# A decay in two factors and a fixed issue order for the first units of a state-space mixer on one Trainium2 core

## Chip, core and metric

The kernel runs on one core of a Trainium2 chip. The metric is the device time in microseconds (us). The engines are TensorE (PE, with its weight loads shown as PEld), VectorE (DVE), ScalarE (ACT), GpSimd (POOL) and SyncE (SP), which here only issues transfers.

## What is computed

Two layers, each an attention-like part and a feed-forward part with residuals and layer norms, over 1024 tokens (4 sequences of 256) of 512 features. The change lies in the second layer's first part, a state-space mixer with 128 heads of 64, 8 groups of state size 128, and chunks of 128 tokens, so two chunks a sequence:

```python
proj = hidden_states @ in_proj_w.T            # gate, hBC (x, B, C), dt
hBC = silu(causal_conv4(hBC) + conv_b)        # depthwise, 4 taps
dt = softplus(dt + dt_bias); A = -exp(A_log)
A_cumsum = cumsum(A * dt)                     # inside each chunk
L = exp(segment_sum(A * dt))                  # decay inside a chunk
Y_diag = (C.B * L) @ (x * dt)                 # a chunk on itself
states = (B * exp(A_cumsum[last] - A_cumsum)).T @ (x * dt)
Y_off = (C @ states of the chunk before) * exp(A_cumsum)
y = Y_diag + Y_off + D * x
out = (y * rsqrt(mean(y*y) + eps) * norm_w * silu(gate)) @ out_proj_w.T
```

With two chunks, only chunk 1 gets anything from before, and that comes from chunk 0. The kernel computes it without states, as a third block of C.B with its own decay. For a token l of chunk 1 and a token s of chunk 0 that decay is exp(cs1[l]) times exp(rev[s]), where cs is the running sum of A dt inside its chunk and rev[s] is the sum of A dt over the tokens of chunk 0 after s.

## The kernel before

Everything is float32. The mixer works through 72 **units**: for each of 8 groups one unit of B and C (units 0, 9, 18, ...), then 8 **pairs** of heads. The main loop at the end of the mixer runs over n, and each turn n does parts of four units:

- `stage_a(n)` projects unit n: seven products (`product`, L503) of two 128x128 by 128x512 matmuls, each of which the trace counts as two instructions. They go into the tiles pd, pa and pb, of a PSUM pool of four buffers (tag "in"). It is Strassen-like: the weights come in two 256 KB loads (win, L558 and L559), GpSimd makes four sums of them (wsum, L489 to L492), ACT copies partial results out of PSUM (`keep`, L514), and DVE adds them to later products (L526, L530, L533). Then DVE makes the causal convolution (`conv_silu`: one instruction L542 and three L546) and ACT the silu (L554). A unit of B and C has two convolutions, a pair has one, and its gate goes through silu on ACT (L591, L592).
- `load_sums(n)` loads the pair's running sums: cst, two rows of cs_d spread over all partitions, two buffers.
- `stage_t(n-1)`: for a unit of B and C, the products C.B of the group (ps_g and p1, L617 and L624), masked into gt by DVE (L634, L640) and ACT (L646). For a pair, transposes of x (ps_xt, L652), x dt (xdt, L655), and the decays in cst: L667 on DVE makes four blocks a head for chunk 0 on chunk 1 out of cst and rev, L671 on ACT eight blocks a head inside the chunks, then one exp over all of it (L675) and two products with gt on DVE (L677).
- `stage_c(n-2)`: ps_y, 16 matmuls a head pair of the blocks inside chunks (L692) and 8 from chunk 0 on chunk 1 (L700), both with xdt as weights; then D, the norm's weight and the gate on DVE (L708, L711), squares on ACT (L710) and their sum (L714).

The output projection (ps_p, L732) adds up to four pairs to two of eight token tiles in every turn, and DVE adds it to acc (L740, L742). The tiles ps_dt, ps_cs, ps_csT, ps_g, ps_xt and ps_y share one PSUM buffer (tag "mm2", one buffer); p1, ps_rev and ps_p share two ("mm1").

Ahead of the loop stands `time_steps`: the dt projection (L405), softplus as a series on DVE (L415 to L433, with a reciprocal, L425), and A dt (adt, L437). At the end of turn 1 `sums` makes the running sums (ps_cs, L445, copied to cs), rev (ps_rev, L454), the transposed sums (ps_csT, L464) and stores them to cs_d in DRAM (L467).

A scheduler orders the instructions of each engine at build time by their place in the program and by its own estimates; each engine then takes its queue in that order, and waits for data and for free buffers with semaphores. Nothing in the program fixes the order beyond the data's own dependencies.

Of the kernel before, what the change touches and what calls it, by code (L numbers as in the profile page):

```python
# [30 lines left out]
P = 128  # L31
# [20 lines left out]
def model_kernel(ctx: ExitStack, tc: tile.TileContext, a: dict, out: bass.AP):  # L52
# [299 lines left out]
    with ExitStack() as c1:  # L352
# [5 lines left out]
        class Psum:  # L358
            @staticmethod
            def tile(shape, dt, tag, name):  # L360
                return {"mm2": psum2, "mm1": psum1, "in": psumi}[tag].tile(shape, dt, tag=tag, name=name)

        wdt = cw.tile([P, KT, P], F32, tag="wdt", name="wdt")
        nc.sync.dma_start(out=wdt, in_=a["win"][T_DT])
# [18 lines left out]
        cs = cw.tile([P, NT, P], F32, tag="cs", name="cs")  # L383
        rev = cw.tile([P, NB, P], F32, tag="rev", name="rev")
        cs_d = dram.tile([P, NTOK], F32, tag="cs_d", name="cs_d")

# [8 lines left out]
        def time_steps():  # L395
# [7 lines left out]
            for t in range(NT):  # L403
                for k in range(KT):
                    nc.tensor.matmul(  # L405
                        flat(ps)[:, toks(t)],
                        lhsT=xnT[:, k, toks(t)],
                        rhs=wdt[:, k, :],
                        start=(k == 0),
                        stop=(k == KT - 1),  # L410
                    )
# [12 lines left out]
            nc.vector.tensor_scalar(r, u, 2.0, None, ALU.add)  # L424
            nc.vector.reciprocal(r, r)  # L425
            nc.vector.tensor_tensor(u, u, r, ALU.mult)
            nc.vector.tensor_tensor(s2, u, u, ALU.mult)
            nc.vector.tensor_scalar(r, s2, 1.0 / 15, None, ALU.mult)
            for n in (13, 11, 9, 7, 5, 3):
                nc.vector.scalar_tensor_tensor(r, r, 1.0 / n, s2, ALU.add, ALU.mult)  # L430
            nc.vector.scalar_tensor_tensor(r, r, 1.0, u, ALU.add, ALU.mult)
# [4 lines left out]
            nc.vector.tensor_scalar(na, na, -1.0, None, ALU.mult)  # L436
            nc.vector.tensor_tensor(adt, dt, bcast_mid(na, sh), ALU.mult)  # L437

            return adt

        def sums(adt):

            ps = Psum.tile([P, 2, 512], F32, "mm2", "ps_cs")
            for n in range(2):
                nc.tensor.matmul(  # L445
                    ps[:, n, :],
                    lhsT=tri_le,
                    rhs=adt[:, n * 4 : n * 4 + 4, :],
                    start=True,
                    stop=True,  # L450
                )
            nc.scalar.copy(cs, flat(ps).rearrange("p (t h) -> p t h", h=P))
            pr = Psum.tile([P, 512], F32, "mm1", "ps_rev")
            nc.tensor.matmul(  # L454
                pr,
                lhsT=tri_gt,
                rhs=adt.rearrange("p (b c) h -> p b c h", c=2)[:, :, 0, :],
                start=True,
                stop=True,
            )  # L460
            nc.scalar.copy(rev, pr.rearrange("p (b h) -> p b h", h=P))
            ps = Psum.tile([P, 2, 512], F32, "mm2", "ps_csT")
            for t in range(NT):
                nc.tensor.transpose(flat(ps)[:, toks(t)], cs[:, t, :], ident)  # L464
            csT = b2.tile([P, NTOK], F32, tag="xdt", name="csT")
            nc.scalar.copy(csT, flat(ps))
            nc.sync.dma_start(out=cs_d, in_=csT)  # L467

# [26 lines left out]
        def project(n, one, two):  # L495
# [4 lines left out]
            def product(ps, wt, tk, start=False):  # L500

                for k in range(2):
                    nc.tensor.matmul(  # L503
                        ps,
                        lhsT=wt[:, k, :],
                        rhs=tk[:, k, :],
                        start=start and k == 0,
                        stop=k == 1,
                        skip_group_check=not start,
                    )  # L510

# [17 lines left out]
            product(pd, v[:, 3], quarter(1, 1))  # L529
            nc.vector.tensor_tensor(one[:, 512:], pd, c2, ALU.add)  # L530
            yield
            product(pa, v[:, 2], tok[2])
            nc.vector.tensor_tensor(two[:, 512:], pa, c3, ALU.add)  # L533
            yield
# [34 lines left out]
        def prefetch(n):  # L569
            if n < len(units):  # L570
# [3 lines left out]
                weight_sums(n)  # L574

        def stage_a(n):
            kind, i = units[n]
# [3 lines left out]
            if kind == "bc":  # L581
                raw2 = xyp.tile([P, NTOK], F32, tag="xy", name=f"raw2_{n}")
                pa = yield from project(n, raw, raw2)
                nc.scalar.copy(raw2[:, :512], pa)
                conv_silu(raw, 64 + i, first)
                conv_silu(raw2, 72 + i, second)
                held[n] = [first, second]
            else:
                pa = yield from project(n, raw, second)
                conv_silu(raw, i, first)  # L590
                nc.scalar.activation(second[:, :512], pa, AF.Silu)  # L591
                nc.scalar.activation(second[:, 512:], second[:, 512:], AF.Silu)  # L592
                held[n] = {"xT": first, "sg": second}
# [3 lines left out]
        def load_sums(n):  # L597

            kind, j = units[n]
            if kind == "bc":  # L600
                return
            cst = b2.tile([P, 2, NT + NB, P], F32, tag="cst", name=f"cst{j}")
            nc.sync.dma_start(
                out=cst.rearrange("p h c l -> p h (c l)")[:, :, :NTOK],
                in_=cs_d[2 * j : 2 * j + 2, :].unsqueeze(0).to_broadcast([P, 2, NTOK]),
            )
            held[n].update(cst=cst)

        def stage_t(n):
            kind, i = units[n]  # L610
            if kind == "bc":
# [4 lines left out]
                for b in range(NB):  # L616
                    nc.tensor.matmul(  # L617
                        flat(ps)[:, b * SEQ : (b + 1) * SEQ],
# [4 lines left out]
                    )  # L623
                    nc.tensor.matmul(  # L624
                        p1[:, toks(b)],
# [25 lines left out]
            for t in range(NT):  # L651
                nc.tensor.transpose(flat(ps)[:, toks(t)], hd["xT"][:, toks(t)], ident)  # L652
            xdt = b2.tile([P, NT, P], F32, tag="xdt", name=f"xdt{j}")
# [5 lines left out]
                ALU.mult,  # L659
            )  # L660


            m = hd["cst"]
            for hh in range(2):
                h = 2 * j + hh
                for b in range(NB):
                    nc.vector.tensor_scalar(  # L667
                        m[:, hh, NT + b, :], m[:, hh, 2 * b + 1, :], rev[:, b, h : h + 1], -1.0, ALU.add, ALU.mult
                    )
                for c in range(NT):  # L670
                    nc.scalar.activation(  # L671
                        m[:, hh, c, :], m[:, hh, c, :], AF.Relu, bias=cs[:, c, h : h + 1], scale=-1.0
                    )
            mf = m.rearrange("p h c l -> p h (c l)")
            nc.scalar.activation(mf, mf, AF.Exp, scale=-1.0)  # L675
            for hh in range(2):
                nc.vector.tensor_tensor(mf[:, hh], mf[:, hh], gr.rearrange("p c l -> p (c l)"), ALU.mult)  # L677
            hd["xdt"] = xdt

        ys = []  # L680

        def stage_c(n):
            kind, j = units[n]
            if kind == "bc":
                return
            hd = held.pop(n)
            xdt, m = hd["xdt"], hd["cst"]
            py = Psum.tile([P, 2, 512], F32, "mm2", f"ps_y{j}")
            for c in range(NT):
                halves = [slice(hh * 64, (hh + 1) * 64) for hh in range(2)]  # L690
                for hh, e in enumerate(halves):
                    nc.tensor.matmul(  # L692
                        flat(py)[e, toks(c)],
# [5 lines left out]
                for hh, e in enumerate(halves if c % 2 else []):  # L699
                    nc.tensor.matmul(  # L700
                        flat(py)[e, toks(c)],
                        lhsT=xdt[:, c - 1, e],
                        rhs=m[:, hh, NT + c // 2, :],
                        start=False,
                        stop=True,
                    )
# [20 lines left out]
        def out_project(q, t, upto):  # L727
# [3 lines left out]
            for j in range(j0, upto):  # L731
                nc.tensor.matmul(  # L732
                    ps,
# [11 lines left out]
        prefetch(1)  # L745
        adt = time_steps()
        token_sums()
        for j in range(6):
            load_wout(j)
        added = 0  # L750
        for n in range(len(units) + 3):
            a_steps = stage_a(n) if n < len(units) else iter(())
            upto, q = len(ys), (len(ys) - 1) % PER_OUT
            fresh = upto > added
            next(a_steps, None)
            if fresh:
                out_project(q, 2 * q, upto)
            next(a_steps, None)
            if 0 <= n - 2 < len(units):
                stage_c(n - 2)  # L760
            next(a_steps, None)
            if fresh:
                out_project(q, 2 * q + 1, upto)
                behind[q] = added = upto
                load_wout(min(behind) + 5) if upto >= PER_OUT else None
            if 0 <= n - 1 < len(units):
                stage_t(n - 1)
            next(a_steps, None)
            if n == 1:
                sums(adt)  # L770
            if n < len(units):
                load_sums(n)
# [115 lines left out]
```

## Time and profile before

| what | value |
|---|---|
| three runs | 1883.59, 1884.53, 1885.9 us |
| median | 1884.53 us |
| profiled execution, its own time | 1885.57 us |
| span of its instructions | 1883.5 us |
| mean granted clock of TensorE | 0.988 |
| PE, DVE, ACT, POOL busy | 1840.0, 1396.1, 1068.8, 308.9 us |
| moved by DMA | 146.63 MB |
| cst, 64 loads of 1024 KB, median to landing | 4.7 us |

The profile is of one execution. A group of instructions has a line, an engine, an operation and its tiles; "idle before" is how long its engine stood still ahead of it and what ended that. A matmul of 128x512 is recorded with its pipeline's end, so four of them in a row last 1.88 us but start again every 1.715 us. The clock column gives the share of TensorE's full clock that was granted.

### The profile page before, as it was taken

How to read it: one execution, taken by the hardware profiler on the slowest of the kernel's cores; microseconds unless marked ns; L12 is line 12 of the kernel's file. 1: busy time of each engine (PE TensorE's matmuls, PEld its weight loads, DVE VectorE, ACT ScalarE, POOL GpSimd, SP SyncE). 2: the span in 40 equal slices, each digit the busy share in tenths (PEclk: the TensorE clock that was granted, in tenths of full speed). 3: DMA queues.
4: the chain of work that ended last, by engine and by line, in shares of the span. 5: the costliest groups of instructions: out<-in, count | busy, mean ns of one | idle time of the engine just before them, and what ended most of it. 6: DMA issues, size and time to landing. Idle time of an engine off the chain costs nothing.

```text
span 1883.5 us, 21008 instructions
## 1 busy us (share of the span) xinstructions
PE 1840.0 (98%) x7726; PEld 965.1 (51%) x7726; DVE 1396.1 (74%) x1924; ACT 1068.8 (57%) x1846; POOL 308.9 (16%) x347
## 2 busy tenths in 40 slices
PE   7999979999999999999999999999999999999999
PEld 4645535454555555554555555555555555555554
DVE  4523788888777878787878777878778777877761
ACT  4311248766566656665666566556666666656630
POOL 5210222222111211111111111111112111211000
PEclk9999989999999999999999999999999999999998
DMA  8100122221222222221222222212221222222211
GB/s 318 56 1 12 51 90 70 88 84 56 85 79 79 79 79 79 79 79 62 79 78 87 82 79 79 78 57 101 79 79 67 73 78 79 79 90 79 79 45 45
DMA packets 56726, 146.63 MB, mean 78 GB/s; under 512 B 5968, under 2 KB 6480, under 8 KB 55472
## 3 DMA queue, kind: packets, MB, share of 16 engines
q1 hardware_dynamic: 54512, 134.00, 20.2%
q0 software_dynamic: 1536, 10.24, 1.4%
q8 instruction: 61, 1.00, 0.2%
q10 hardware_dynamic: 576, 1.05, 0.2%
q14 instruction: 41, 0.34, 0.1%
HBM read 140.55 MB, written 4.72 MB: 77 GB/s over the span
## 4 chain that ended last, share of the span: by engine, by line
PE 86%; DVE 8%; ACT 3%; issue 1%; DMA 1%; ACTq 0%; DVEq 0%; SPq 0%
PE pa L503 23%; PE ps_p L732 21%; PE pd L503 11%; PE ps_y L692 6%; PE pb L503 6%; PE f_pso L171 3%; PE ps_q L94 3%; PE ps_o L306 3%; PE ps_xt L652 3%; PE ps_y L700 3%; DVE xT L546 2%; DVE cst L677 1%; PE f_psl L157 1%; ACT cst L675 1%; PE ln_ps L121 1%
## 5 line engine op out<-in xcount | busy, mean ns | idle before, releaser
L732 PE MATMUL ps_p<-wout,xT 128*128 128x512 f32 x1024 | 461.3, 593 | 0.0
L671 ACT ACTIVATE cst<-cst,cs 128x128 f32<-128x128 f32 x1024 | 330.5, 391 | 127.5 <-DMA cst<-cs_d 79.8
L732 PEld LDWEIGHTS ps_p<-wout,xT 128*128 128x128 f32 x1024 | 193.9, 190 | 242.4 <-issue 238.0
L489 POOL TENSOR_TENSOR wsum<-win 128x256 f32<-128x256 f32 x72 | 70.3, 977 | 1276.3 <-PE pa L503 760.5
L546 DVE SCALAR_TENSOR_TENSOR xT<-raw,convw,xT 128x1020 f32<-128x1020 f32 (+2 forms) x216 | 277.5, 1285 | 1.4
L677 DVE TENSOR_TENSOR cst<-cst,gt 128x1536 f32<-128x1536 f32 x128 | 222.2, 1764 | 73.4 <-ACT cst L675 72.5
L710 ACT ACTIVATE sq<-xT 128x1024 f32<-128x1024 f32 x64 | 67.7, 1057 | 299.2 <-DVE xT L708 299.2
L675 ACT ACTIVATE cst<-cst 128x3072 f32<-128x3072 f32 x64 | 176.9, 2764 | 0.7
L742 DVE TENSOR_TENSOR acc<-ps_p,acc 128x512 f32<-128x512 f32 x126 | 86.3, 685 | 117.6 <-PE ps_p L732 117.5
L692 PE MATMUL ps_y<-cst,xdt 128*64 128x128 f32 x2048 | 159.7, 276 | 2.0 <-issue 2.0
L667 DVE TENSOR_SCALAR cst<-cst,rev 128x128 f32<-128x128 f32 x512 | 156.4, 367 | 0.0
L503 PE MATMUL pa<-xnT,wsum 128*128 128x512 f32 x288 | 141.9, 615 | 4.5 <-ACT keep L514 4.5
L692 PEld LDWEIGHTS ps_y<-cst,xdt 128*64 128x64 f32 x2048 | 118.6, 137 | 52.1 <-issue 40.7
L503 PE MATMUL pd<-tok,wsum 128*128 128x512 f32 x288 | 136.7, 593 | 1.4 <-POOL wsum L489 1.4
L503 PE MATMUL pd<-xnT,wsum 128*128 128x512 f32 x288 | 136.5, 596 | 0.9 <-ACT keep L514 0.9
L503 PE MATMUL pa<-tok,wsum 128*128 128x512 f32 x288 | 136.2, 595 | 0.0
L503 PE MATMUL pa<-tok,win 128*128 128x512 f32 x288 | 135.9, 594 | 0.3 <-DVE sg L533 0.3
L503 PE MATMUL pa<-xnT,win 128*128 128x512 f32 x288 | 135.8, 592 | 0.2 <-DVE raw L526 0.2
L503 PE MATMUL pb<-xnT,win 128*128 128x512 f32 x288 | 135.3, 592 | 0.0
L514 ACT COPY keep<-pa 128x512 f32<-128x512 f32 x144 | 82.9, 576 | 50.4 <-PE pa L503 49.6
L526 DVE TENSOR_TENSOR raw<-pb,keep 128x512 f32<-128x512 f32 x72 | 49.5, 688 | 80.2 <-PE pb L503 80.0
L700 PE MATMUL ps_y<-cst,xdt 128*64 128x128 f32 x1024 | 101.1, 273 | 0.0
(176 smaller groups left out, 2442.7 us busy)
## 6 DMA issues: line engine op xcount, KB each, us to landing
cst<-cs_d SPq DMA_DIRECT2D x64, 1024.0 KB, 4.7
win<-in_win SPq DMA_DIRECT2D x144, 256.0 KB, 2.8
wout<-in_wout SPq DMA_DIRECT2D x64, 256.0 KB, 2.7
wo_s<-in_wo POOLq DMA_DIRECT2D x8, 1024.0 KB, 5.3
wq<-in_wq SPq DMA_DIRECT2D x8, 256.0 KB, 5.1
x_d<-x SPq DMA_DIRECT2D x8, 256.0 KB, 2.0
xr<-x_d SPq DMA_DIRECT2D x2, 1024.0 KB, 5.6
out<-acc SPq DMA_DIRECT2D x8, 256.0 KB, 2.0
```

The costliest lines, as they stand in the source:

```text
L489: op(v[:, 0], w[:, 1, 0:2], w[:, 1, 2:4], ALU.add)
L503: nc.tensor.matmul(ps, lhsT=wt[:, k, :], rhs=tk[:, k, :], start=start and k == 0, stop=k == 1, skip_group_check=not start,)
L514: nc.scalar.copy(c, ps)
L546: nc.vector.scalar_tensor_tensor(d[:, :, k:], src[:, :, : SEQ - k], convw[:, i, TAPS - 1 - k : TAPS - k], d[:, :, k:], ALU.mult, ALU.add,)
L667: nc.vector.tensor_scalar(m[:, hh, NT + b, :], m[:, hh, 2 * b + 1, :], rev[:, b, h : h + 1], -1.0, ALU.add, ALU.mult)
L671: nc.scalar.activation(m[:, hh, c, :], m[:, hh, c, :], AF.Relu, bias=cs[:, c, h : h + 1], scale=-1.0)
L675: nc.scalar.activation(mf, mf, AF.Exp, scale=-1.0)
L677: nc.vector.tensor_tensor(mf[:, hh], mf[:, hh], gr.rearrange("p c l -> p (c l)"), ALU.mult)
L692: nc.tensor.matmul(flat(py)[e, toks(c)], lhsT=xdt[:, c, e], rhs=m[:, hh, c, :], start=True, stop=c % 2 == 0,)
L700: nc.tensor.matmul(flat(py)[e, toks(c)], lhsT=xdt[:, c - 1, e], rhs=m[:, hh, NT + c // 2, :], start=False, stop=True,)
L732: nc.tensor.matmul(ps, lhsT=ys[j][:, toks(t)], rhs=wouts[j], start=(j == j0), stop=(j == upto - 1),)
L742: nc.vector.tensor_tensor(acc[:, t, :], ps, acc[:, t, :], ALU.add)
```

## The change

**The decay from chunk 0 in two factors.** exp(cs1[l] + rev[s]) is no longer made in cst by L667. Its factor exp(rev[s]) goes, with dt, into a new tile `dtr` (once, 128x4x128), and each pair makes `xdr`, the chunk-0 part of x times dtr, beside xdt. The factor exp(cs1[l]) comes ready from DRAM: cs_d has 512 more columns with chunk 1's sums, and is stored with the sign turned, so the loads of cst are 1536 KB in place of 1024 KB, one exp covers all 12 blocks as before, and L671's scale changes its sign. The matmuls of L700 take xdr as weights.

**The order at the first units.** A table `early` says which steps run where in turns 0 to 4; `turn` puts them behind PE's last instruction so far, and further products of `project` behind them in turn ("bar"). `issue_after` adds an edge of order between instructions on one engine, without a semaphore. `time_steps` is a generator whose three parts come behind the last adds of units 0 and 1. The convolutions of units 0 and 1 are set aside (`later`): unit 0's first comes behind A dt, its second behind the add `one` of unit 2, unit 1's behind the add `two` of unit 2; those of unit 2 and later are not set aside. `sums` goes from turn 1 to turn 2 and is split into `first_sums` and `spread_sums`; the first C.B goes from turn 1 to turn 3, together with the transposes of unit 1; ps_y of units 1 and 2 both come in turn 4, and the output projection may then take up two new pairs in one turn.

```diff
@@ sums
-            nc.scalar.copy(rev, pr.rearrange("p (b h) -> p b h", h=P))
+            nc.scalar.activation(dtr, pr.rearrange("p (b h) -> p b h", h=P), AF.Exp)
+            nc.vector.tensor_tensor(
+                dtr, dtr, dt.rearrange("p (b c) h -> p b c h", c=2)[:, :, 0, :], ALU.mult
+            )
+        def spread_sums(_):
...
-            nc.scalar.copy(csT, flat(ps))
-            nc.sync.dma_start(out=cs_d, in_=csT)
+            nc.scalar.activation(csT, flat(ps), AF.Identity, scale=-1.0)
+            nc.sync.dma_start(out=cs_d[:, :NTOK], in_=csT)
+            nc.sync.dma_start(
+                out=cs_d[:, NTOK:].rearrange("h (b l) -> h b l", l=P), in_=chunks(csT)[:, :, 1, :]
+            )
@@ product
-                for k in range(2):
-                    nc.tensor.matmul(
+                with issue_after(last["bar"]):
+                    for k in range(2):
+                        last["pe"] = nc.tensor.matmul(
@@ stage_a
-                conv_silu(raw, 64 + i, first)
-                conv_silu(raw2, 72 + i, second)
+                later(n, lambda: conv_silu(raw, 64 + i, first))
+                later(n, lambda: conv_silu(raw2, 72 + i, second))
...
-                conv_silu(raw, i, first)
+                later(n, lambda: conv_silu(raw, i, first))
@@ load_sums
-                out=cst.rearrange("p h c l -> p h (c l)")[:, :, :NTOK],
-                in_=cs_d[2 * j : 2 * j + 2, :].unsqueeze(0).to_broadcast([P, 2, NTOK]),
+                out=cst.rearrange("p h c l -> p h (c l)"),
+                in_=cs_d[2 * j : 2 * j + 2, :].unsqueeze(0).to_broadcast([P, 2, (NT + NB) * P]),
@@ stage_t
+            xdr = b2.tile([P, NB, P], F32, tag="xdr", name=f"xdr{j}")
+            nc.vector.tensor_tensor(
+                xdr.rearrange("p b (h e) -> p b h e", e=64),
+                flat(ps).rearrange("p (b c h e) -> p b c h e", c=2, h=2, e=64)[:, :, 0],
+                bcast(dtr[:, :, 2 * j : 2 * j + 2], [P, NB, 2, 64]),
+                ALU.mult,
+            )
...
-                for b in range(NB):
-                    nc.vector.tensor_scalar(
-                        m[:, hh, NT + b, :], m[:, hh, 2 * b + 1, :], rev[:, b, h : h + 1], -1.0, ALU.add, ALU.mult
-                    )
                 for c in range(NT):
                     nc.scalar.activation(
-                        m[:, hh, c, :], m[:, hh, c, :], AF.Relu, bias=cs[:, c, h : h + 1], scale=-1.0
+                        m[:, hh, c, :], m[:, hh, c, :], AF.Relu, bias=cs[:, c, h : h + 1], scale=1.0
@@ stage_c
-                        lhsT=xdt[:, c - 1, e],
+                        lhsT=xdr[:, c // 2, e],
@@ main loop
+        def more_steps(_):
+            with issue_after(last["two"]):
+                adt.append(next(steps))
+
+        def convolve(tile):
+            n, behind_this = tile
+            with issue_after(last[behind_this]):
+                delayed[n].pop(0)()
...
+        early = {
+            0: ([], [], [(more_steps, 0)]),
+            1: ([], [], [(more_steps, 0), (convolve, (0, "adt"))]),
+            2: ([], [(first_sums, 0), (convolve, (0, "one"))], [(convolve, (1, "two")), (spread_sums, 0), (load_sums, 1)]),
+            3: ([], [(stage_t, 0), (stage_t, 1)], []),
+            4: ([(stage_t, 2)], [(stage_c, 1)], [(stage_c, 2), (stage_t, 3)]),
+        }
+
+        def turn(n, i):
+            if n not in early:
+                step, m = [(None, 0), (stage_c, n - 2), (stage_t, n - 1)][i]
+                if step and 0 <= m < len(units):
+                    step(m)
+            elif early[n][i]:
+                with issue_after(last["pe"]):
+                    for step, m in early[n][i]:
+                        step(m)
+                last["bar"] = last["pe"]
...
-            fresh = upto > added
+            fresh = [(upto, (upto - 1) % PER_OUT) for upto in range(added + 1, len(ys) + 1)]
...
-            if n < len(units):
+            if 1 < n < len(units):
                 load_sums(n)
```

## The prediction, made before the changed kernel was run

> **What bounds the kernel now.** I read the busy shares, then the slices, then TensorE's waits, then windows over the gap that they show.
>
> ```profile
> PE 1840.0 (98%) x7726; PEld 965.1 (51%) x7726; DVE 1396.1 (74%) x1924; ACT 1068.8 (57%) x1846; POOL 308.9 (16%) x347
> ...
> PE   7999979999999999999999999999999999999999
> ...
> PEclk9999989999999999999999999999999999999998
> ```
>
> TensorE (PE) works all the time but for the first slice and the sixth (235 to 282 us), where the granted clock dips too: the mixer's first units. Its own waits there (us in total, times, longest):
>
> ```profile
> PE ps_g L617 <- ACT sg L554: 10.5, 1, 10.5
> PE ps_y L692 <- issue: 2.0, 1, 2.0
> PE pd L503 <- POOL wsum L489: 1.4, 2, 0.9
> PE pd L503 <- ACT keep L514: 0.9, 1, 0.9
> ```
>
> Busy us of PE, PEld, DVE, ACT, POOL, then the granted clock, in windows:
>
> ```profile
> 217.00:239.00 22.00, 21.77 (x52) 9.19 (x51) 20.38 (x17) 7.29 (x10) 2.34 (x2) 1.00 0.07 24
> 239.00:268.00 29.00, 17.96 (x52) 10.24 (x51) 23.33 (x22) 8.35 (x11) 8.50 (x8) 0.76 0.10 37
> 268.00:298.00 30.00, 26.21 (x110) 13.26 (x109) 22.34 (x33) 23.49 (x45) 2.94 (x4) 0.94 0.32 122
> 298.00:346.00 48.00, 47.71 (x212) 24.28 (x212) 47.18 (x62) 39.78 (x76) 16.70 (x12) 1.00 0.22 78
> ...
> 550.00:600.00 50.00, 50.00 (x212) 25.33 (x211) 38.93 (x51) 31.13 (x55) 5.66 (x8) 1.00 0.29 100
> ```
>
> From 218 us VectorE (DVE) has some 23 us of softplus (one 6.55 us reciprocal, the rest of 0.7 or 1.2) and 9.2 us of unit 0's two convolutions (0.81 + 3 x 1.27 each), interleaved; C.B (ps_g, L617) stands in PE's queue ahead of everything later and waits for both, 10.5 us. From 500 to 1800 every window has PE busy 50.00 of 50: what DVE saves there is worth nothing. The whole prize lies between 240 and 500 us. I measure it by the start of each unit's first product, pd<-tok:
>
> ```profile
> 240.51 1.98 PE L503 MATMUL pd<-tok,wsum 128*128 128x512 f32 x4 [0.57 <-POOL wsum L489]
> ...
> 357.04 1.88 PE L503 MATMUL pd<-tok,wsum 128*128 128x512 f32 x4
> 380.76 1.88 PE L503 MATMUL pd<-tok,wsum 128*128 128x512 f32 x4
> 403.49 1.88 PE L503 MATMUL pd<-tok,wsum 128*128 128x512 f32 x4
> ```
>
> The second line is unit 7's. By then the kernel has done the same matmuls before and after the change: projections 0 to 6, sums, C.B, transposes of units 1 to 5, ps_y of units 1 to 4, 12 output products.
>
> **What the Trainium skill says.** *TensorE: Matmul & The Clock Gate*, "What's actually happening": after an idle window of about 3.4 us PE runs at half clock until it has been busy for such a window. The trace agrees: after the 10.5 us wait the clock is 0.50 and ps_g takes 5.28 us (252.97 to 258.25), in a later group 2.62 (1038.82 to 1041.44). *SBUF — State Buffer*, "Who interferes with whom": a DVE instruction with two SBUF inputs and a GpSimd one that reads SBUF block each other. Here L546 goes from 1.27 to 1.75 us and GpSimd's sums from 0.73 to 1.71 where they meet. *DMA: Bandwidth & Descriptors*, "Anatomy of one DMA — SWDGE (gpsimd) path": 2.0 us and bytes at 436 GB/s. These transfers are on the hardware queue, but 256 KB in 2.8 us (win) and 1024 KB in 4.7 us (cst) have the same slope, 2.5 us a MB.
>
> **The change, part by part.** Baseline of the sum: the profiled execution, 1885.57 us (span 1883.5, 2.07 around it), 1.04 above the median 1884.53.
>
> *Decay in two factors.* L667 goes: 512 at 0.305 us, 156.4 us of DVE. Added: 64 products xdr, 128x512 out of PSUM; the nearest row is L640, 0.68 us: 43.5 us (bounds 0.62 to 0.75). DVE falls by 113 us, 1.8 a pair. No PE work changes: the 1024 matmuls of L700 read xdr instead of xdt. On the path: nothing from 500 us on; in 298 to 346, where DVE is busy 47.18 of 48, it counts, and it is in the walk below. ps_xt's one PSUM buffer is freed 0.6 us later; ps_y needs it some 14 us later: nothing.
>
> *Transfers.* Each cst load grows from 1024 to 1536 KB, 64 times. At the slope above it lands in 6.0 us, +1.3 (bounds: 0, if the fixed part rules; +2.4, in proportion). ScalarE (ACT) already waits for it (79.8 us over 39 times), and keeps stand in its queue behind the wait. In pair units that is hidden: keep of pa ends at 1112.80, the product that needs it starts at 1116.58. At the first pair after a B,C unit the new queue puts exp (2.77) and a second table load (1.28, *ScalarE: Activation LUTs*, "What ACT_TABLE_LOAD costs"; the same in the trace) ahead of that keep: walking it, it ends at 1033.3 where PE comes at 1033.56. Seven such places, 0 to 0.8 us each; I take 1 us in all. csT is written twice, the second time 256 KB in pieces of 512 B: 2.0 us (x_d) to 5; I take 3.0.
>
> *The first units.* I walked the built kernel's queues from 239.7 us (same state in both: only unit 1's last product open), each instruction when its engine is free and its inputs are there. Cadences from the trace: product of 4 instructions 1.715 us, ps_y 2.77, ps_xt 0.88, L430 and L546 1.22 and 1.27, less 0.08 before an independent one, plus 0.04 before a dependent one, 1.5 us on DVE for each set of GpSimd sums. PE's work to pd of unit 7: 36 products 61.7, C.B 2.6, sums and transposes 3.45, ps_xt 4.4, ps_y 11.1, 12 output products 10.3: 93.5 us. Before, it took 357.04 − 239.70 = 117.3: 23.8 lost.
>
> After: DVE's L552 of unit 1 waits for PE until 239.9; then come n=7, max, n=5, na, n=3, two steps and A dt: 0.60 + 1.14 + 0.61 + 1.14 + 0.22 + 3 x 1.26 + 1.21 = 8.7, with 1.5 for GpSimd 250.1. PE has projected unit 2 by 250.07, so ps_cs waits 0.1. From 250.1 DVE has four convolutions (unit 0's two, units 1 and 2: 17.6), four adds to PSUM products 2.4, dtr 0.5, GpSimd 1.5: unit 2's is done at 272.1. Unit 0's second is silu'd at 263.3 and C.B is due at 267.3: the 10.5 us wait is gone. The edges give order on one engine and no semaphore, so a wait is only where data or a buffer is late. What is late next:
> - unit 2's last product waits for L552, in DVE's queue behind convolutions: 1.2; a keep: 0.45.
> - ps_xt of unit 1 at 269.9. It needs C.B's PSUM buffer (one), whose last reader is the gt copy on ACT. That copy is queued behind cst 0's first relu (load issued about 261.9 behind win 4 on SP's queue, landing 268 to 269; win 5 is queued behind it) and silu of unit 2 (DVE ready at 272.1). Copy done at 274.1: 4.3 us idle. Behind it wait all products.
> - pd of unit 5 waits for GpSimd's sums of win 5, which could load only when unit 3 ended: 1.0.
> - ps_y of unit 2 waits for its exp and product with gt: 1.7.
> - Catching up with two pairs in one turn: ps_xt of unit 3 0.8, output product waits for DVE to empty one 2.1, ps_xt of unit 4 1.25, rest 0.2.
>
> Sum 13.1, pd of unit 7 at 346.3: 10.7 earlier. The 4.3 us gap should cost half clock for one window, and a second gap may: −2.0 (bounds 0 and 3.4). Added table loads (Exp between Silus, 2 x 1.28) fall into waits of ACT. Later: before loses 1.0 in unit 7 (23.72 against 22.73 a unit) and 1.9 in 400 to 500 us (49.43 and 48.64 of 50), as DVE is behind; in the walk DVE at unit 7 waits for PE, so this 2.9 is recovered but for 0.5. The end of the kernel stays.
>
> Sum: 10.7 − 2.0 + 2.9 − 0.5 − 1.0 = 10.1. The profiled time would be 1875.5, the median 1874.5.
>
> **Rivals.**
> - *The moved waits vanish* (0.15): if silu of unit 2 and the gt copy come before ps_xt is due (GpSimd's sums shift, so DVE is not stretched), its 4.3 and the clock's 2.0 go: 16.4 gained, 1868. For: the scheduler put them in that order. Against: DVE is a full queue until 272.
> - *The stall moves more than it shrinks* (0.15): the cst 0 load lands late (pieces of 512 B, win 4 ahead on the same queue) or DVE is stretched more; each us beyond 270.2 delays copy, ps_xt and all that follows. 3 us late and half clock twice: 5 gained, 1879.5.
> - *Slower: ACT's keeps behind the longer loads* (0.07). If 1536 KB lands later than 4.7 + 1.3 + 4 = 10 us, keep of pa misses its product in every pair unit, and each further us costs 62. 0.3 a unit is 18.6, less the 10.1: 1893. For: 79.8 us of such waits are there now. Against: DMA engines are busy 0.2 of the time.
> - *The walk* (0.63): 1869 to 1880.
>
> **Numbers.** Measurement tells about 0.2% from no change, 3.8 us: 1880.8 to 1888.3. Faster: 0.15 + 0.61 of the walk + half of the moved stall = 0.83; same 0.11; slower 0.06. The range, 1865 to 1884, takes in the first two rivals, and leaves out the third and their tails.
>
> **What would show it.** ps_g without a wait; one wait of about 4 us at ps_xt of unit 1 released by the gt copy; unit 7's pd near 346; PE still 50.00 of 50 in later windows; DVE near 1283 us; cst landing near 6.0. Wrong if later windows fall under 50, if ps_cs waits long for adt, or if the first ps_y waits.

## The result, and the profile after

The changed kernel takes 1870.22 us, the kernel before 1885.22 us in the same comparison (6 runs each): ratio 0.9919, 95% interval 0.9906 to 0.9931, 15.0 us faster, less than 1%. Predicted were 1874.5 us, 10.1 us faster. The time lies in the range; the gain is half as large again as the sum.

Busy shares and slices of the changed kernel:

```profile
PE 1833.9 (98%) x7726; PEld 958.0 (51%) x7726; DVE 1292.7 (69%) x1477; ACT 1068.3 (57%) x1848; POOL 308.1 (16%) x347
...
PE   7999989999999999999999999999999999999999
...
PEclk9999999999999999999999999999999999999998
```

The hole of the sixth slice is nearly closed. TensorE's own waits between 200 and 500 us (us in total, times, longest):

```profile
PE ps_xt L679 <- ACT gt L673: 4.3, 1, 4.3
PE ln_ps L121 <- DVE xn L118: 1.9, 1, 1.9
PE pd L522 <- POOL wsum L507: 1.7, 2, 0.9
PE pa L522 <- DVE sg L552: 1.4, 2, 1.2
PE ps_p L761 <- DVE acc L769: 1.2, 1, 1.2
```

ps_g no longer stands there, and in its place stands one wait of 4.3 us at ps_xt of unit 1, released by the gt copy (the second line lies ahead of unit 0). Windows (busy PE, PEld, DVE, ACT, POOL, then the granted clock):

```profile
239.00:268.00 29.00, 26.22 (x76) 12.73 (x74) 28.66 (x29) 13.32 (x17) 13.16 (x7) 1.00 0.41 148
268.00:298.00 30.00, 26.26 (x111) 13.89 (x112) 22.10 (x22) 25.50 (x47) 3.85 (x6) 0.94 0.25 95
298.00:346.00 48.00, 45.92 (x244) 24.52 (x244) 44.27 (x44) 44.54 (x82) 10.25 (x8) 1.00 0.35 127
...
400.00:450.00 50.00, 50.00 (x216) 26.28 (x215) 40.29 (x39) 32.48 (x55) 9.97 (x8) 1.00 0.27 95
450.00:500.00 50.00, 50.00 (x217) 25.67 (x216) 35.77 (x37) 26.29 (x52) 6.64 (x10) 1.00 0.31 106
```

From 239 to 268 us PE works 26.2 us in place of 18.0 and DVE is full; from 400 to 500 us PE no longer waits. First products of units 7, 8 and 9:

```profile
343.73 1.88 PE L522 MATMUL pd<-tok,wsum 128*128 128x512 f32 x4
366.92 1.88 PE L522 MATMUL pd<-tok,wsum 128*128 128x512 f32 x4
389.65 1.88 PE L522 MATMUL pd<-tok,wsum 128*128 128x512 f32 x4
```

Unit 7 comes at 343.7; the walk put it at 346.3, without the half clock. But unit 0 itself starts at 213.06 us, and before at 216.86, behind code that is the same in both. So I cut every profile at the starts of units 0 and 7 and at the end of the span:

| profile | unit 0 starts at | from 0 to 7 | from 7 to the end | unit 0 to the end |
|---|---|---|---|---|
| before | 216.86 | 140.18 | 1526.46 | 1666.64 |
| before, again (e_before) | 215.73 | 140.16 | 1526.41 | 1666.57 |
| changed | 213.06 | 130.67 | 1524.17 | 1654.84 |
| changed, again (e_after2) | 213.81 | 130.24 | 1523.05 | 1653.29 |
| e_decay | 214.46 | 139.22 | 1522.82 | 1662.04 |
| e_order | 214.43 | 130.53 | 1525.74 | 1656.27 |
| e_noedges | 212.79 | 130.46 | 1524.15 | 1654.61 |
| e_gtfirst | 218.17 | 132.77 | 1523.86 | 1656.63 |
| e_gtfix | 213.93 | 128.47 | 1524.00 | 1652.47 |
| e_fill | 212.76 | 126.15 | 1523.09 | 1649.24 |
| e_warm | 211.41 | 127.28 | 1524.01 | 1651.29 |
| e_relief | 213.37 | 127.46 | 1526.87 | 1654.33 |
| e_both | 211.72 | 127.51 | 1524.27 | 1651.78 |

Of the 15.66 us between the two first profiles, 3.80 lie ahead of unit 0, 9.51 between units 0 and 7, and 2.29 behind unit 7 (3.03 gained up to 500 us, 0.74 lost at one late keep).

### The profile page after: what moved, and what is told of

Read it like the earlier page. It is cut to its first block, busy times and chain, and to the rows that moved or that the text cites. A ratio compares the mean times of both kernels' runs of the same rounds, so it can differ in the third digit from the quotient of the medians.

```text
span 1867.9 us, 20526 instructions
## 1 busy us (share of the span) xinstructions
PE 1833.9 (98%) x7726; PEld 958.0 (51%) x7726; DVE 1292.7 (69%) x1477; ACT 1068.3 (57%) x1848; POOL 308.1 (16%) x347
## 3 DMA queue, kind: packets, MB, share of 16 engines
q0 software_dynamic: 1536, 10.24, 1.4%
## 4 chain that ended last, share of the span: by engine, by line
PE 93%; DVE 3%; ACT 2%; DMA 1%; issue 0%; POOL 0%; SPq 0%; DVEq 0%; ACTq 0%; POOLq 0%
PE pa L522 26%; PE ps_p L761 23%; PE pd L522 12%; PE ps_y L721 6%; PE pb L522 6%; PE f_pso L171 3%; PE ps_xt L679 3%; PE ps_q L94 3%; PE ps_o L306 3%; PE ps_y L729 3%; PE f_psl L157 1%; DMA cst<-cs_d 1%; PE ln_ps L121 1%; PE ps_n L278 1%; PE ps_g L644 1%; PE f_pso L190 1%
## 5 line engine op out<-in xcount | busy, mean ns | idle before, releaser
L701 ACT ACTIVATE cst<-cst,cs 128x128 f32<-128x128 f32 x1024 | 326.5, 397 | 88.6 <-DMA cst<-cs_d 78.9
L507 POOL TENSOR_TENSOR wsum<-win 128x256 f32<-128x256 f32 x72 | 79.1, 1099 | 1265.1 <-DMA win<-in_win 637.3
L721 PE MATMUL ps_y<-cst,xdt 128*64 128x128 f32 x2048 | 160.3, 276 | 0.0
L729 PE MATMUL ps_y<-cst,xdr 128*64 128x128 f32 x1024 | 101.9, 273 | 0.0
L573 ACT ACTIVATE xT<-xT 128x1024 f32<-128x1024 f32 x72 | 76.3, 1060 | 31.9 <-DVE xT L565 31.8
```

The lines of the kernel that those rows point to most:

```text
L507: op(v[:, 0], w[:, 1, 0:2], w[:, 1, 2:4], ALU.add)
L573: nc.scalar.activation(dst, dst, AF.Silu)
L701: nc.scalar.activation(m[:, hh, c, :], m[:, hh, c, :], AF.Relu, bias=cs[:, c, h : h + 1], scale=1.0)
L721: last["pe"] = nc.tensor.matmul(flat(py)[e, toks(c)], lhsT=xdt[:, c, e], rhs=m[:, hh, c, :], start=True, stop=c % 2 == 0,)
L729: last["pe"] = nc.tensor.matmul(flat(py)[e, toks(c)], lhsT=xdr[:, c // 2, e], rhs=m[:, hh, NT + c // 2, :], start=False, stop=True,)
```

## The experiments

### Both kernels once more (e_before, e_after2)

No edit.

> The kernel before, unchanged, for a second profile and the clock of each run. In the two profiles at hand the first product of unit 0 starts at 216.86 us before and 213.06 us after, although the code ahead of it is the same; before shows half clock there behind three waits of about 2 us, after doesn't. Theory A (which waits bring half clock differs from execution to execution): the new profile has this start somewhere between 213 and 217 us, not at 216.9 again with the same three places, and the clock varies from run to run. Theory B (it belongs to the program): 216.9 again, half clock at the same three places, and every run of before has a lower clock than every run of after.

> The changed kernel, unchanged, for a second profile and the clock of each run. From the start of unit 0 to the end the two profiles of before last 1666.6 us each and the changed one 1654.8, so 11.8 of the 15.0 us are certain; the rest is in the start of unit 0, which code that is the same in both reaches at 216.9 and 215.7 us before and at 213.1 after. Theory A (chance of the half-clock windows): the new profile ends 1654.8 after unit 0's start again, and that start lies anywhere between 213 and 217 us; runs spread over 1868 to 1873. Theory B (the program decides): unit 0's start at 213 again and no run over 1871.

Measured: before 1884.31 us (14 runs, 1879.80 to 1887.92, clock 0.987 to 0.993); changed 1869.83 us (5 runs, 1869.12 to 1873.52, clock 0.992 to 0.995), which is 13.9 us faster than the 9 runs of before in its own comparison, ratio 0.9929 (0.9917 to 0.9942). From unit 0 to the end before repeats within 0.1 us and the changed kernel within 1.6. Of these 1.6 us, 0.4 lie between units 0 and 7 (its wait at ps_xt was 3.8 us this time) and 1.1 near the end of the kernel, where the clock stays at half for 13.7 us in place of 17.1. Ahead of unit 0, the clock in stretches of 8 us around three waits of some 2 us, first before, then changed (the clock is the column after POOL):

```profile
88.00:96.00 8.00, 6.02 (x39) 5.73 (x38) 4.67 (x15) 3.48 (x7) 0.00 (x0) 0.79 0.01 2
154.00:162.00 8.00, 5.53 (x36) 5.39 (x35) 3.19 (x11) 2.75 (x4) 1.26 (x1) 0.79 0.00 1
203.00:211.00 8.00, 5.31 (x26) 4.28 (x25) 5.28 (x15) 2.54 (x6) 2.53 (x4) 0.79 0.67 188
```

```profile
88.00:96.00 8.00, 5.88 (x44) 4.78 (x43) 5.07 (x16) 4.91 (x9) 0.00 (x0) 1.00 0.01 2
154.00:162.00 8.00, 6.21 (x54) 6.22 (x55) 3.12 (x14) 2.16 (x3) 1.27 (x1) 1.00 0.00 1
203.00:211.00 8.00, 6.76 (x58) 6.47 (x59) 6.15 (x11) 2.75 (x6) 4.50 (x5) 1.00 0.50 137
```

The waits are equally long (1.84, 2.47, 1.95 us in both). Before, each brought half clock, and the stretches from one wait to the next, and from the last to unit 0, are 1.32, 1.43 and 1.53 us longer (the changed kernel had lost 0.48 us more ahead of them, which leaves 3.80); in the changed kernel none did. The second profile of before shows it at two of them, e_order and e_decay at one each, e_noedges at none, and e_gtfirst, which is the changed kernel but for one edge, at all three. So which waits bring it isn't fixed by the program: the start of unit 0 lay between 212.8 and 218.2 us in the profiles of kernels that don't touch this stretch. The clock records fit this: in every profile half clock lasts 3.41 us or a whole multiple of it (but for the stretch that the end of the trace cuts). Where a wait falls in a grid of such windows may then decide; no run tests that. The first profile of before had drawn three, that of the changed kernel none. That explains the difference of the two profiles. It doesn't explain why the medians are 13.9 to 15.0 us apart: unit 0 to the end accounts for 11.7 to 13.4 us. The remaining 0.5 to 3.3 us stay open: they may be chance of few runs, or something in the programs may favour one alignment. Half clock stood behind 5 of the 6 such waits in the two profiles of before and 7 of the 24 in the eight of the changed kernel and its variants that leave this stretch alone, too few to decide.

### The two halves of the change (e_decay, e_order)

e_decay is the kernel before with the decay in two factors (cs_d, dtr, xdr, the sign, L667 gone) and nothing of the order; e_order is the changed kernel with the decay of before:

```diff
-            nc.scalar.activation(dtr, pr.rearrange("p (b h) -> p b h", h=P), AF.Exp)
+            nc.scalar.copy(rev, pr.rearrange("p (b h) -> p b h", h=P))
...
+                for b in range(NB):
+                    nc.vector.tensor_scalar(
+                        m[:, hh, NT + b, :], m[:, hh, 2 * b + 1, :], rev[:, b, h : h + 1], -1.0, ALU.add, ALU.mult
+                    )
...
-                        lhsT=xdr[:, c // 2, e],
+                        lhsT=xdt[:, c - 1, e],
```

> Only the decay in two factors, in the order of before. Theory: the 10.5 us wait at ps_g stays, nothing is gained up to it; what DVE saves (1.8 us a pair) gives back what before lost in catching up, 3.0 us behind unit 7 and up to 3 before it, less 0.7 for one late keep: 2 to 6 us faster, 1879 to 1883. Rival (DVE's load is the whole matter): 10 us or more faster. Second rival (the longer loads of cst cost more without the new order, since the pair units stand tighter): slower by 1 us or more.

> Only the order, with the decay of before (512 instructions on DVE, loads of 1024 KB). Theory: ps_g without a wait, 4 us at ps_xt of unit 1; the cst load is shorter, so that its first relu comes a little earlier; but DVE has 1.8 us a pair more and must catch up after 270 us, so that the later loss of 3 us stays and 2 to 4 us more come in 285 to 345 us: 7 to 11 us faster than before, 1874 to 1878. Rival (the order is the whole gain): 14 us or more faster. With e_decay the two gains should add to 15 within 3 us; a sum much under it would mean that the parts need each other.

Measured: e_decay 1877.48 us (0.9962, 0.9950 to 0.9974), 7.3 us faster than before; e_order 1874.18 us (0.9943, 0.9931 to 0.9955), 10.6 us faster. e_decay gained more than the 2 to 6 us expected; from unit 0 on it is 4.6 us, inside them. Neither rival holds. The table says what each half does. The order alone brings 0 to 7 from 140.18 to 130.53, as in the changed kernel (130.67 and 130.24): on balance the decay is worth nothing there. That is a balance of two things, not proof that DVE's time is free. In e_order the input of silu of unit 2, which DVE makes, is ready 55.3 us after unit 0's start, in the changed kernel after 54.0; but there the first relu waits for the longer cst load until 55.4, and in e_order the load, 1024 KB, has landed after 51.1. No run separates the two. The expected 2 to 4 us of loss from 285 to 345 us did not come. The decay alone leaves ps_g's 10.5 us:

```profile
PE ps_g L623 <- ACT sg L560: 10.5, 1, 10.5
```

Its gain lies behind unit 7, 3.64 of 4.60 us: there before lost time around the second unit of B and C (units 10 to 12 start 25.36 and 21.38 us apart before, 25.44 and 21.38 in e_order, 24.47 and 19.76 in e_decay and in the changed kernel). So most of each half's gain lies in a stage of its own. They are not quite independent: their cuts from unit 0 on add to 15.0, the whole measured 11.8 and 13.3. One part of that shows: the changed kernel loses 0.7 us at a late keep behind unit 7, and e_decay, with the same loads, at none.

### Without the edges (e_noedges)

```diff
         def issue_after(ins):
-            return tc.issue_after(ins.ins) if ins else nullcontext()
+            return nullcontext()
```

> The changed kernel with every edge of order taken out: the steps stand in the same place in the program, but the scheduler may move them. It then mixes unit 0's convolutions with softplus again on DVE (A dt some 7 us later, about 252 us), and puts ps_cs two products later on PE (about 250 us); on ACT the gt copy comes ahead of cst 0's relu. Theory: PE waits some 2 us for A dt at ps_cs, but the 4.3 us at ps_xt of unit 1 shrink: within 3 us of the changed kernel, 1867 to 1873. Rival (the edges carry the gain): 8 us or more of it are lost, 1878 or more.

Measured: 1869.51 us (0.9922, 0.9911 to 0.9934), as the changed kernel. The waits are others (between 214 and 520 us):

```profile
PE ps_y L721 <- DVE cst L707: 5.0, 1, 5.0
PE ps_cs L454 <- DVE adt L447: 0.9, 1, 0.9
```

The wait at ps_xt is gone, and ps_y of the first pair waits for the cst product 5.0 us instead. The theory holds in time, and A dt was 0.9 us late in place of 2. The gain comes from the place of the steps in the program; the edges choose which wait is left, and here both choices cost the same.

### The gt copy first (e_gtfirst, e_gtfix)

```diff
-                nc.scalar.copy(gt[:, NT:, :], chunks(flat(ps))[:, :, 1, :])
+                last["gt"] = nc.scalar.copy(gt[:, NT:, :], chunks(flat(ps))[:, :, 1, :])
...
+                with issue_after(last["gt"] if n == 1 else None):
                     for c in range(NT):
```

> One more edge: on ACT the relus of unit 1 come behind the gt copy, so the copy no longer stands behind the first cst load. Theory (the 4.3 us at ps_xt of unit 1 are the copy's place in ACT's queue, and only partly the data): silu of unit 2 has its input at 267.1, so the copy runs at 268.2 and ps_xt starts at 268.8 in place of 270.9: the wait shrinks to 2.2 us, and DVE's own read of ps_g (ends 268.2) is next. 2 us faster than the changed kernel, up to 4 where the half clock after the gap goes as well: 1866 to 1868.5. Rival (ps_y of unit 1 or another wait takes the time): 1869.5 to 1871, the 2 us come back before unit 7.

Measured: 1875.04 us (0.9953, 0.9941 to 0.9966), slower than the changed kernel, the rival's side, and worse. From unit 0 on it is 1.8 to 3.3 us slower (1656.6 us); the rest of the 5 us lies elsewhere, in part ahead of unit 0, where its profile had half clock at all three waits. ACT of the changed kernel around the copy shows what the edge takes away:

```profile
268.43 0.69 ACT L701 ACTIVATE cst<-cst,cs 128x128 f32<-128x128 f32 x2 [3.27 <-DMA cst<-cs_d]
269.03 1.04 ACT L573 ACTIVATE xT<-xT 128x1024 f32<-128x1024 f32 x1
269.98 0.39 ACT L701 ACTIVATE cst<-cst,cs 128x128 f32<-128x128 f32 x1
270.27 0.56 ACT L673 COPY gt<-ps_g 128x512 f32<-128x512 f32 x1
```

The copy's input was there at 266.6; it stood behind relus that waited for a load until 268.4. With the edge the wait at ps_xt fell to 2.3 us, as expected. But:

```profile
PE pd L522 <- DVE acc L770: 4.5, 1, 4.5
PE ps_xt L679 <- ACT gt L673: 2.3, 1, 2.3
```

DVE in the same kernel, some 40 us later:

```profile
311.89 3.42 DVE L708 TENSOR_TENSOR cst<-cst,gt 128x1536 f32<-128x1536 f32 x2
315.23 1.28 DVE L770 COPY acc<-ps_p 128x512 f32<-128x512 f32 x2
```

The edge on ACT also moved what the scheduler puts where on DVE: two cst products now stand ahead of the copies that empty ps_p. PE stands 4.5 us, and behind that the clock is at half for two windows (6.8 us). e_gtfix makes unit 3's products behind such a copy:

```diff
+            if n == 3:
+                put_off.append(masked)
...
             for upto, q in fresh:
                 out_project(q, 2 * q, upto)
+            if n == 5:
+                put_off.pop()()
```

(`masked` holds the two products under `issue_after` the last copy.)

> The kernel with the gt copy first again, which was slower though its wait at ps_xt fell from 4.3 to 2.3 us. In its trace DVE makes unit 3's two cst products (3.4 us) ahead of the copies of ps_p out of PSUM, and PE then stands 4.5 us until such a copy; in the changed kernel the copies came first and PE stood 1.2 us. Here the two products come behind the copy of ps_p of tile 2, as in the changed kernel. Theory (that swap is the whole loss): PE's wait for a copy falls from 4.5 to about 1 us, and from unit 0's start to the end it takes 1652 to 1653 us, against 1656.6 with the swap and 1654.8 and 1653.3 in the two profiles of the changed kernel. Rival (the earlier relus load DVE and ACT otherwise): 1655 us or more still.

Measured: 1867.47 us (0.9912, 0.9897 to 0.9927), and 1652.5 us from unit 0 on; the wait for a copy is 1.2 us. So the swap, with the half clock behind it, was the loss. The gt copy's place is worth 0.8 to 2.4 us against the two profiles of the changed kernel. Behind the shorter wait ps_xt runs at full clock:

```profile
269.77 1.09 PE L679 MATMUL ps_xt<-ident,xT 128*128 128x128 f32 x8 [2.32 <-ACT gt L673]
```

So from unit 0 to unit 7 the wait gives 2.0 us and the half clock that is gone 1.9, and 1.7 us more go to the GpSimd sums (3.4 in place of 1.7): 2.2 together, as the table has it (130.67 and 128.47).

### Filler in the gap (e_fill)

```diff
+            if n == 1:
+                pf = Psum.tile([P, 512], F32, "mm1", "ps_fill")
+                with issue_after(last["pe"]):
+                    for _ in range(4):
+                        last["pe"] = nc.tensor.matmul(pf, lhsT=ident, rhs=quarter(0, 1)[:, 0], start=True, stop=True)
+            with issue_after(last["pe"] if n == 1 else None):
...
```

> Four products that nobody reads are put into the 4.3 us gap between C.B and ps_xt of unit 1 (3.4 us of PE work at full clock), so that PE is busy there; the gap itself stays. It measures the half clock's price alone. Theory: ps_xt starts at 270.9 as before, takes 0.88 in place of 1.85 us, and the product behind it no longer starts late: 1.9 us less, 1868.3. Rival (half clock comes from something else than the idle time, or its price is hidden by the later wait on the GpSimd sums): no change within 0.5 us. If the filler itself delays ps_xt, its start shows it.

Measured: 1866.70 us (0.9909, 0.9896 to 0.9923). The gap in the changed kernel, then the filled one:

```profile
270.88 1.85 PE L679 MATMUL ps_xt<-ident,xT 128*128 128x128 f32 x8 [4.30 <-ACT gt L673]
272.53 2.84 PE L522 MATMUL pa<-xnT,wsum 128*128 128x512 f32 x4
```

```profile
266.31 3.60 PE L682 MATMUL ps_fill<-xnT,ident 128*128 128x512 f32 x8
269.78 1.09 PE L685 MATMUL ps_xt<-ident,xT 128*128 128x128 f32 x8
270.71 1.88 PE L522 MATMUL pa<-xnT,wsum 128*128 128x512 f32 x4
```

ps_xt and the product behind it took 1.85 and 2.84 us, and take 1.09 and 1.88: the half clock cost 1.7 to 1.9 us. The profile gains 4.5 us between units 0 and 7, not 1.9: ps_xt also starts 0.8 us earlier after unit 0, and the later waits are 1.6 us shorter (0.6 and 0.8 in place of 0.9, 0.9 and 1.2). The median gains 3 us. The three profiles with a wait of 3.8 to 4.3 us at ps_xt (changed, e_after2, e_order) all have half clock behind it, and the four with fillers (this one and the three below) have none.

### Later loads (e_slowcst)

```diff
+            if n > 4:
+                nc.sync.dma_start(
+                    out=more.rearrange("p (h l) -> p h l", h=2),
+                    in_=cs_d[2 * j : 2 * j + 2, :].unsqueeze(0).to_broadcast([P, 2, (NT + NB) * P]),
+                )
```

(`more` is a scratch in DRAM.)

> Ahead of each cst load from unit 5 on, another 1536 KB go from the same place in DRAM to a scratch in DRAM on the same queue; the result isn't touched. It puts the prediction's third rival to the test: how far the loads may slip before ACT's keeps are late. At 2.5 us a MB cst should land at about 10 us in place of 6.2. In the changed kernel's profile the second keep of pa ends 2.5 us before PE needs it in a unit whose cst landed 7.2 us after its issue. Theory (slack 2.5 us, so the limit is near 9.7 us, where the prediction put 10): at 10 us PE loses 0.3 to 1 us in most of 60 units, 20 to 60 us slower. Rival (ACT or the order of the queue gives way, keeps are not late): within 3 us of the changed kernel.

Measured: 1913.03 us (1.0149, 1.0135 to 1.0163), 43 us slower than the changed kernel. The extra transfers wait for nothing and run ahead, some three for each load until 800 us, and none after. Issues from 500 to 600 us:

```profile
more<-cs_d SPq DMA_DIRECT2D x12, 1536.0 KB, 8.1
cst<-cs_d SPq DMA_DIRECT2D x4, 1536.0 KB, 11.8
```

From 300 to 800 us, 20 loads land after 10.1 to 11.8 us (medians of 100 us), and PE waits for keeps (300 to 900 us):

```profile
PE pa L523 <- ACT keep L534: 25.9, 9, 8.1
```

From 900 us on, with 6.2 us, PE waits for nothing. So keeps are late, as the theory has it, but in some 20 units and not in most of 60, and they are not alone: of 35 us that PE lost from 300 to 800 us, 27 are waits for keeps, the rest waits for DVE, and half clock came on top. 43 us over 20 units are 2.1 us each at about 11 us. A rough estimate, if each further us costs one: the limit is near 9 us, 1 below the prediction's and 2.8 above what the change needs.

### Filler ahead of unit 0, relief of DVE, and both (e_warm, e_relief, e_both)

e_warm is e_fill with, in a layer norm and ahead of a ps_n, products into the PSUM tile that is used next:

```diff
+    def warm(ps, rhs, count):
+        with tc.issue_after(latest[0].ins):
+            for _ in range(count):
+                latest[0] = nc.tensor.matmul(ps, lhsT=ident, rhs=rhs, start=True, stop=True)
...
+        if warm_with is not None:
+            warm(ps, warm_with, 2)
```

(A ps_n is a PSUM tile of the attention-like part.) e_relief has e_gtfirst's edge, three fillers in place of four, and

```diff
+            if i in (64, 72):
+                nc.scalar.activation(
+                    d, src, AF.Identity, bias=convb[:, i : i + 1], scale=convw[:, i, TAPS - 1 : TAPS]
+                )
...
```

e_both is the sum of the two.

> The kernel with the filler products in the gap, and two more such products in each of two waits of about 2 us far ahead of unit 0 (at 91 and 155 us), in code that the change doesn't touch. Theory (half clock behind these waits is chance, and is most of the spread between runs): no half clock at these two places, unit 0's start below 214.2 us in the profile, runs closer together than the 5 us of the kernel with the filler alone, median 1 to 2.5 us lower: 1864.2 to 1865.7. Rival (the spread comes from elsewhere, or fillers delay the work behind them): median within 0.5 us of 1866.7 or higher.

> A version meant to be faster: unit 0's two first taps of the convolution go from DVE (0.81 us each) to ACT, the gt copy comes ahead of the first relu, and three filler products (2.6 us) stand in the gap that is left. DVE should have L549 of unit 2 behind it 1.4 us earlier and ps_xt of unit 1 starts right behind the filler, 0.9 us earlier than with four. Theory: from unit 0's start to the end 1648 to 1649 us, against 1649.2 with four fillers and 1654.8 for the changed kernel; time 1864.5 to 1866.5. Rival (the next limit, DVE's copies or the GpSimd sums, takes it): 1650 us or more.

> The two before put together: relief of DVE, gt copy first, three fillers in the gap, and the fillers in the two waits ahead of unit 0. Theory: the effects add, 1863 to 1865 us, with the lowest spread of runs. Rival: as in either of the two alone.

Measured: e_warm 1865.06 us (0.9900, 0.9886 to 0.9915; 4 runs, 1864.78 to 1866.90), e_relief 1866.96 (0.9911, 0.9896 to 0.9926), e_both 1865.78 (0.9905, 0.9888 to 0.9921). The clock of e_warm at the two filled waits is 1.00:

```profile
88.00:96.00 8.00, 7.86 (x45) 5.39 (x45) 4.18 (x14) 4.98 (x8) 0.00 (x0) 1.00 0.01 2
154.00:162.00 8.00, 7.94 (x69) 7.74 (x68) 3.25 (x16) 1.87 (x2) 1.28 (x1) 1.00 0.00 1
```

Unit 0 starts at 211.4 and 211.7 us with these fillers, earlier than in every other profile, and the runs of e_warm lie within 2.1 us. That fits the theory of e_warm, but doesn't show it: without fillers half clock stood at these two places in 8 of 24 cases only, so none in 4 can be chance, and the 4 runs of e_gtfix, without any filler, lie within 2.4 us. e_relief missed, on its rival's side (1654.3 us from unit 0 on): ps_xt came earlier, but unit 7 no earlier than in e_fill and e_warm, and as in e_both. Behind unit 7 it took 2.6 us more than e_both; 0.8 of them are waits at ps_p, and about 1.2 come near the end, where half clock lasts 20.5 us in place of 17.1. e_both missed as well: the effects do not add. e_warm has the lowest median: its 4 runs all lie below the 11 runs of the changed kernel (1868.69 to 1873.52). It can't be told from e_fill, e_relief and e_both, whose intervals overlap its own.

## Why the prediction was right, and where its sum was off

**The wait at ps_g.** Right: gone. From unit 0 to unit 7 the kernel gains 9.51 us, where 10.7 − 2.0 = 8.7 were predicted.

**The wait at ps_xt.** Right in place and size, 4.3 against 4.30 us, for a reason that was half wrong. The walk let the copy wait for silu of unit 2, whose input it put at 268.3 us (on the changed profile's scale, 3.8 us earlier), and held the cst 0 load for decisive only if it landed beyond 266.4. Silu's input was ready at 267.0, and the load landed at 268.4, 9.8 us after its issue at 258.5: the step "landing 268 to 269", 6 to 7 us after issue, had it too short. Three other loads were under way on the same queue: win 4 (two of 256 KB, issued 0.5 and 0.9 us ahead) and cst 1 (1536 KB, issued 0.4 us behind). In e_noedges the same two cst loads go together, but win 4 had landed before, and cst 0 lands after 6.9 us. So win 4, which the walk had named, goes with most of the delay, and cst 1 with 0.7 us of it; no run changes one of them alone. e_gtfirst confirms the load's part of the wait: 2.0 of the 4.3 us. The second rival's mechanism (cst 0 late) was thus at work, without its price, since silu had been put too late.

**The other waits.** The walk gave 13.1 us; the gaps in the slices from 239 to 346 us sum to 8.6. Right were L552 (1.2, measured 1.18) and the sums of win 5 (1.0, 0.85). Too large: the keep (0.45, 0.19) and the output product (2.1, 1.21). Not there at all: ps_y of unit 2 (1.7), ps_xt of units 3 and 4 (0.8, 1.25). Not foreseen: the sums of win 6 (0.87). Against this the work itself was taken too short. With the same number of PE instructions before and after (485 and 484 in the trace), PE is busy 121.83 us from unit 0 to unit 7, 119.9 without the half clock; the cadences of the walk gave 22.84 + 93.5 = 116.3. Two things make up most of the 3.6 us. At some 18 places, next to a ps_y or behind a wait, a product takes 0.1 us more (1.82 from start to start in place of 1.72; behind ps_xt, C.B or the sums it takes 1.72). And the ends of the pipeline ahead of the seven waits, 0.16 us each, count as busy. The two errors, 4.5 and 3.6 us, nearly cancelled: that the total came out so close is in part luck.

**Half clock.** Right: −2.0, measured 1.9 in the changed profile and 1.7 to 1.9 by e_fill.

**Later losses.** 2.9 − 0.5 were predicted, 3.03 measured: 0.53 in unit 7, the rest around the second unit of B and C. The cause given, DVE being behind, holds for the second part, and e_order and e_decay show that it is the decay that cures it, not the order. The prediction's sentence that saved DVE time "counts" in 298 to 346 us isn't borne out: on balance the decay changed nothing up to unit 7, and its two sides there weren't separated.

**Loads and keeps.** Right: landing 6.2 us (6.0 predicted), the second csT write 3.2 us (3.0), one of seven places lost, 0.74 us (1.0 in all). The third rival's limit of 10 us may be nearer 9, by the estimate above. DVE fell by 103 us (113 predicted): xdr is 43.8 us as taken, but the three later steps of the convolutions of C went from 1.28 to 1.48 us each and some smaller rows grew.

**What the sum lacked.** It was made against one execution, and took the rest of that execution as fixed. The weak step is "Baseline of the sum: the profiled execution": 3.80 of the 15.66 us between the profiles lie ahead of unit 0, in half clock behind waits that were there before and after. The other 11.86 compare with 10.1: 0.8 from the walk, 0.6 from the later losses, 0.3 from the keep, the rest rounding. Against the second profile of the changed kernel it is 13.3.

## What to carry to other kernels

Where a queue holds a product that waits for a full engine, walk the queues of all engines over that stage alone and ask of each engine what stands behind the wait that is late next: here a copy stood behind relus that waited for a load, and one edge added there shifted another engine's order for a loss of 4.2 us (e_gtfirst against e_gtfix, from unit 0 on). Cut each profile at a place that both kernels reach with the same work done, before a difference of whole times is explained: a quarter of the difference of the two profiles (3.80 of 15.66 us) lay in code that had not been touched. An idle gap that can't be closed can be filled: behind the 4.3 us gap, products that nobody reads kept the clock up.

## What the runs showed of the hardware

Waits of 1.84, 2.47 and 1.95 us on PE brought half clock in some executions and not in others, with the same program and the same lengths (three, two, one or none of three places), at 1.3 to 1.5 us each. *TensorE: Matmul & The Clock Gate*, "What's actually happening", speaks of an idle window of about 3.4 us; these waits are shorter than that, so here the measurement decides. Among the mixer's first units, waits of 3.8 to 10.5 us brought it in all eight profiles that have one; waits of 2.3 us (e_gtfirst, e_gtfix) and one of 3.6 us (e_slowcst) did not. All half-clock stretches behind these waits last 3.4, 6.8, 10.2 or 13.7 us, multiples of 3.41.

Two cst loads of 1536 KB issued together, 0.5 us behind two loads of 256 KB on the same queue, landed 9.8 and 13.0 us after their issue; without the two smaller loads ahead (e_noedges) 6.9 and 10.2; single ones take 6.2.
